# Second norm's tiles of two sequences turned by 32x32 blocks through DRAM, and two early norms moved

## The chip, the cores and the metric

One core of one Trainium2 chip runs the whole program in one launch. The metric is device time in microseconds (us). The engines named are TensorE (PE; its weight loads are shown apart as PEld), VectorE (DVE), ScalarE (ACT), GpSimd (POOL), and SyncE (SP), which here does nothing but issue transfers.

## The reference

Four sequences of 512 tokens with 512 features, float32. A sequence mixing block is followed by an MLP block, each behind a layer norm and with a residual:

```
x = x + attention(layernorm(x))
x = x + mlp(layernorm(x))

attention, 4 heads of 128, chunks of 128 tokens:
  q, k, v = projections of x; k normalised per head
  alpha = sigmoid(...), beta = softplus(...)
  cla = cumsum(log(alpha)) in the chunk
  attn = (q k^T) * beta * exp(cla - cla^T), lower triangle
  y = attn v + (q state) * exp(cla)
  state = state * exp(cla_end) + v^T (k * beta * exp(cla_end - cla))

mlp:  Wg, Wu, Wd dequantised from 4-bit codes and scales, 4096 hidden
  out = (gelu(x Wg^T) * (x Wu^T)) Wd^T
```

## The kernel before, in words

There are B = 4 sequences with NCH = 4 tiles of 128 tokens each, 16 tiles in all. A matrix product needs its features on the partitions, so every normalised tile of 128 tokens by 512 features has to be turned. For the MLP a float32 activation is also split into three parts (hi, lo, mi) that multiply separately.

**Steps.** The attention runs as a counted list of steps p, 12 for each sequence: four of `product_v`, four of `product_q`, four of `product_k`. After the projection of a step, `behind(p)` (L775) emits the chunk work that is due. Chunk (b, n), the n-th of sequence b, gets the three steps from 9 + 3(4b + n) on, so it runs beside the projections of a later sequence. Among those three, p % 3 = 0 prepares the decay, which needs a broadcast load of cumulated gate sums (`load_sums`, L579) and gives the mask `dm`; p % 3 = 1 turns what is waiting (`turn("f")`, `turn("a")`), makes `chunk_scores` and multiplies them with `dm` (L674), and issues loads; p % 3 = 2 makes the chunk's output `yp` (`chunk_sums`, L717 and L719), adds it to the residual tile and stores the sum (`accd`, L727), and in `rest()` starts the next chunk's values and calls `second_norm`. Then come the early `first_norm` calls that the table `early` (L739 to L743) holds for this p, and `settle()`. Each engine works through its instructions in the order in which they are emitted.

**The norms.** `norm` (L330) takes statistics on DVE (L334, L338, L340), an inverse root on POOL (L341), and leaves the rest to `settle()` (L343). There are two ways to turn:

- *On PE.* DVE scales the tile in one operation (L359), and `turn` later transposes four 128x128 blocks into a PSUM bank `tp` (L380), and hands it to `use`.
- *By blocks.* DVE scales it in two halves into an order of 32-column pieces (L349). `cross` (L307) writes the tile (256 KB) to DRAM from SP (L310). One step later SP reads it back in four pieces of 64 KB (L315), so that each 32x32 block lands where it belongs but for its own transposition; three steps after that, at the end of the step, DVE transposes within the blocks (`turn_blocks`, L320, L326). The dictionaries `first_of` and `last_of` hold what is due at the start and at the end of a step.

`first_norm` (attention input, key "a") goes by blocks for all sequences but the first and on PE for that. Some keys of sequences 0 to 2 go by blocks also (way_k). `second_norm` (MLP input, key "f", L402) goes on PE for all 16 tiles. Its `use` takes hi with ACT (L406), lo and mi with DVE (L407, L408), and stores the three from SP to DRAM (`h<-g`, L410); the MLP loads them from there (`x<-h`).

**SP** issues nearly all transfers, in the emitted order. An instruction of SP that waits holds everything behind it.

**The MLP** runs in rounds over slices of 128 hidden columns, and overlaps the end of the attention from about 180 us on.

Of the kernel before, what the change touches and what calls it, by code (L numbers as in the profile page):

```python
# [35 lines left out]
def f32(t):  # L36
    return t.bitcast(F32)
# [3 lines left out]
def tile_gated_linear_attention__then__nvfp4_geglu(  # L41
# [22 lines left out]
    NCH = T // P  # L64
# [56 lines left out]
    one_k = Homes("b", 42, [P, T], two_k)  # L121
# [4 lines left out]
    def heads(t):  # L126
        return t.rearrange("p (h d) -> p h d", d=P)
# [176 lines left out]
    def crossed(t):  # L304
        return t.rearrange("p (w k i) -> p k w i", w=KC, i=32)

    def cross(src, key, use, landing, turning):  # L307

        way = dram.tile([KC, P, P], F32, tag=f"way_{key}", name=f"way_{key}")
        nc.sync.dma_start(way.rearrange("w p m -> p w m"), f32(src).rearrange("p (w m) -> p w m", m=P))  # L310

        def land():
            t = one_k.get(f"way_{key}")
            for a in range(KC):
                nc.sync.dma_start(f32(t)[:, a * P : (a + 1) * P], way[:, a * 32 : (a + 1) * 32, :])  # L315
            last_of.setdefault(turning, []).append(lambda: use(t))

        first_of.setdefault(landing, []).append(land)

    def turn_blocks(t, *to):  # L320

        new = f32(t).rearrange("p (a k i) -> p k a i", a=KC, i=32)
        done = 0
        for part in to:
            n = part.shape[1]
            nc.vector.transpose(part.rearrange("p k (a j) -> p k a j", j=32), new[:, done : done + n])  # L326
            done += n
        one_k.put(t)

    def norm(src, key, use, parts=1, within=None, way=None):  # L330


        st = small.tile([P, 6], F32, tag="st", name=f"st_{key}")
        nc.vector.bn_stats(st, f32(src))  # L334
        if within:
            within()
        mv = small.tile([P, 2], F32, tag="mv", name=f"mv_{key}")
        nc.vector.bn_aggr(mv, st)  # L338
        rs = small.tile([P, 1], F32, tag="rs", name=f"rs_{key}")
        nc.vector.tensor_scalar(rs, mv[:, 1:2], 1e-5, None, ALU.add)  # L340
        nc.gpsimd.tensor_tensor(rs, rs, minus_half[:, :1], ALU.pow)  # L341

        def settle():  # L343

            hn = one_k.get(f"hn_{key}")
            w = D // parts
            if way:
                for c in range(2):
                    nc.vector.tensor_scalar(  # L349
                        crossed(f32(hn)).rearrange("p (c two) w i -> p c two w i", c=2)[:, c],  # L350
                        f32(src).rearrange("p (c w i two) -> p c two w i", c=2, w=KC, two=2)[:, c],
                        mv[:, 0:1], rs, ALU.subtract, ALU.mult,
                    )
                one_k.put(src)
                cross(hn, key, way, place[0] + 1, place[0] + 4)
                one_k.put(hn)
                return
            for cols in (slice(i * w, (i + 1) * w) for i in range(parts)):
                nc.vector.tensor_scalar(  # L359
                    f32(hn)[:, cols].rearrange("p (c two j) -> p c two j", two=2, j=P),  # L360
                    f32(src)[:, cols].rearrange("p (c j two) -> p c two j", two=2, j=P),
                    mv[:, 0:1], rs, ALU.subtract, ALU.mult,
                )
            one_k.put(src)
            turned.append((hn, key, use))

        settled.append(settle)
# [34 lines left out]
    def second_norm(b, n, src):  # L402
        def use(tp):
            g = [one_k.get(f"g{j}_{b}_{n}") for j in range(3)]
            hi, lo, mi = g
            nc.scalar.activation(hi, tp, AF.Copy, scale=HI)  # L406
            nc.vector.tensor_tensor(lo, tp, f32(hi), ALU.subtract)  # L407
            nc.vector.scalar_tensor_tensor(mi, f32(hi), ONE_E, tp, ALU.mult, ALU.subtract)  # L408
            for j in range(3):
                nc.sync.dma_start(  # L410
                    h2d[b][j][:, :, n * P : (n + 1) * P].rearrange("k p t -> p k t"), heads(f32(g[j]))
                )
            one_k.put(*g)

        norm(src, f"f{b}_{n}", use)


    zs, ss = {}, {}
# [289 lines left out]
    def chunk_sums(b, n):  # L708
        add = state_sums(b, n) if b < B - 1 else None
        old = ch.pop("old")  # L710
        one_k.put(v_sb.pop((b, n)))
        dm, vb = ch.pop("dm"), ch.pop("vb")
        qc = ch.pop("qc", None)
        yp = psum(f"yp_{b}_{n}")
        for h in range(H):
            hs = slice(h * P, (h + 1) * P)
            nc.tensor.matmul(yp[:, hs], f32(dm)[:, hs], f32(vb)[:, hs], start=True, stop=(n == 0))  # L717
            if n > 0:
                nc.tensor.matmul(yp[:, hs], f32(qc)[:, hs], f32(old)[:, hs], start=False, stop=True)  # L719
        one_k.put(dm, vb)  # L720
        if n > 0:
            one_k.put(qc, old)
        a = acc.pop((b, n))

        def sums():
            nc.vector.tensor_tensor(f32(a), f32(a), yp, ALU.add)  # L726
            nc.sync.dma_start(accd[b * NCH + n], f32(a))  # L727

        def rest():
            if n + 1 < NCH:  # L730
                chunk_values(b, n + 1)
            second_norm(b, n, a)
            if add:
                add()

        return sums, rest
# [2 lines left out]
    early = {}  # L739
    for b in range(1, B):  # L740
        for n in range(NCH):
            p = 3 * NCH * (b - 1) + 3 * n - 1 if b > 1 else 2 + 3 * min(n, 2)
            early.setdefault(p, []).append((b, n))  # L743
    xs = {}

# [253 lines left out]
    with tc.manual_schedule():  # L999
# [45 lines left out]
        p = 0  # L1045
# [95 lines left out]
```

## Time and profile before

| | us |
|---|---|
| median of 3 runs | 1303.85 (1300.8 to 1305.99) |
| the profiled execution's own time | 1303.89 |
| its span | 1302.2 |

Busy time of each engine over the span:

| engine | us | what is in it |
|---|---|---|
| PE | 1289.4 | 1139 are the MLP's products (L853, L897) |
| DVE | 968.9 | MLP sums and the unpacking of its weights |
| ACT | 452.0 | |
| POOL | 113.6 | nearly all in the first 270 us |

A row of the groups reads: line, engine, operation, output<-inputs, shapes, count | busy us, mean ns of one | idle time of the engine just ahead of it and what ended it. Some rows that bear on the turning:

| row | count | mean ns |
|---|---|---|
| L359 DVE, tile scaled in one (tiles of "f") | 16 | about 546 |
| L349 DVE, half of a tile scaled | 16 in 57 to 175 us | 501 (406 where nothing is beside it) |
| L326 DVE, block transposes of 128x256 | 24 | 404 |
| L326 DVE, of 128x512 | 6 | 701 |
| L310 SP, issue of a write | 18 | 380 |
| L315 SP, issue of a read | 72 | 522 |
| L410 SP, issue of a store of h | 48 | 418 |

In the chain of waits each piece is start, length, and what it was; "SPq" is the time that SP spent on issuing.

### The profile page before, as it was taken

How to read it: one execution, taken by the hardware profiler on the slowest of the kernel's cores; microseconds unless marked ns; L12 is line 12 of the kernel's file. 1: busy time of each engine (PE TensorE's matmuls, PEld its weight loads, DVE VectorE, ACT ScalarE, POOL GpSimd, SP SyncE). 2: the span in 40 equal slices, each digit the busy share in tenths (PEclk: the TensorE clock that was granted, in tenths of full speed). 3: DMA queues.
4: the chain of work that ended last, by engine and by line, in shares of the span. 5: the costliest groups of instructions: out<-in, count | busy, mean ns of one | idle time of the engine just before them, and what ended most of it. 6: DMA issues, size and time to landing. Idle time of an engine off the chain costs nothing.

```text
span 1302.2 us, 17046 instructions
## 1 busy us (share of the span) xinstructions
PE 1289.4 (99%) x5736; PEld 1032.0 (79%) x5736; DVE 968.9 (74%) x1581; ACT 452.0 (35%) x878; POOL 113.6 (9%) x179
## 2 busy tenths in 40 slices
PE   9999999999999999999999999999999999999998
PEld 6567676778888888888888888888888888887886
DVE  3577865888777777777777777777777777777566
ACT  2333335743333333333333333333333333332332
POOL 1536362400000000000000000000000000000000
PEclk9999999999999999999999999999999999999999
DMA  5457677987565656555656565555555555555473
GB/s 195 147 178 195 191 197 214 301 268 235 178 194 178 194 178 194 178 194 179 194 179 193 179 193 179 192 180 192 180 191 181 189 183 189 183 178 198 167 252 127
DMA packets 195383, 250.24 MB, mean 192 GB/s; under 512 B 16672, under 2 KB 93792, under 8 KB 195296
## 3 DMA queue, kind: packets, MB, share of 16 engines
q1 hardware_dynamic: 195296, 249.16, 59.2%
q8 instruction: 45, 0.74, 0.2%
q14 instruction: 42, 0.34, 0.1%
HBM read 191.91 MB, written 57.18 MB: 191 GB/s over the span
## 4 chain that ended last, share of the span: by engine, by line
PE 93%; DMA 3%; DVE 2%; SPq 1%; ACT 1%; issue 0%; POOL 0%; DVEq 0%; ACTq 0%; POOLq 0%
PE pa L853 35%; PE p_d L897 26%; PE pb L853 18%; PE pq L450 4%; PE pk L474 2%; PE pva L425 2%; PE pvb L432 2%; PE yp L717 1%; PE sp L663 1%; PE yp L719 1%; DMA x<-in_x 1%; PE dp L688 1%; DMA pk_d<-in_down_p 1%; PE tp_f L380 0%; DMA x<-h 0%
## 5 line engine op out<-in xcount | busy, mean ns | idle before, releaser
L853 PE MATMUL pa<-x,wgu 128*128 128x512 f32 x2048 | 507.2, 390 | 0.0
L853 PEld LDWEIGHTS pa<-x,wgu 128*128 128x128 f32 x2048 | 384.1, 188 | 79.0
L897 PE MATMUL p_d<-wd,i 128*128 128x512 f32 x1542 | 357.2, 389 | 2.3 <-DVE xr L726 0.6
L897 PEld LDWEIGHTS p_d<-wd,i 128*128 128x128 f32 x1542 | 288.3, 188 | 65.6 <-DVE i L877 2.1
L853 PE MATMUL pb<-x,wgu 128*128 128x512 f32 x1024 | 274.7, 390 | 1.8 <-DMA x<-h 1.8
L858 ACT ACTIVATE t<-pb 128x512 f32<-128x512 f32 x256 | 151.3, 591 | 358.0 <-PE pb L853 353.4
L859 DVE TENSOR_TENSOR t<-pa,t 128x512 f32<-128x512 f32 x256 | 176.6, 690 | 81.2 <-ACT t L858 75.9
L853 PEld LDWEIGHTS pb<-x,wgu 128*128 128x128 f32 x1024 | 192.4, 188 | 42.4 <-DMA x<-h 2.5
L905 DVE SCALAR_TENSOR_TENSOR acc<-p_d,acc 128x512 f32<-128x512 f32 (+1 forms) x137 | 93.4, 682 | 124.8 <-PE p_d L897 123.7
L873 ACT ACTIVATE i<-t 128x512 fp32r<-128x512 f32 x128 | 81.0, 633 | 194.2 <-DVE t L870 189.7
L865 ACT ACTIVATE t<-t 128x512 f32<-128x512 f32 x128 | 81.2, 634 | 136.6 <-DVE t L859 136.5
L877 DVE TENSOR_TENSOR i<-t,i 128x512 fp32r<-128x512 f32 x128 | 88.4, 691 | 25.9 <-ACT i L873 24.1
L909 DVE TENSOR_TENSOR acc<-acc,p_d 128x512 f32<-128x512 f32 x135 | 93.0, 689 | 14.8 <-PE pb L853 0.5
L870 DVE SCALAR_TENSOR_TENSOR t<-t,t 128x512 f32<-128x512 f32 x128 | 88.6, 692 | 4.3
L928 POOL TENSOR_TENSOR acc<-acc,last 128x512 f32<-128x512 f32 x1 | 1.3, 1295 | 1015.0 <-ACT last L927 1015.0
L878 DVE SCALAR_TENSOR_TENSOR i<-i,t 128x512 fp32r<-128x512 f32 x128 | 89.0, 695 | 0.0
L450 PE MATMUL pq<-hT,wq 128*128 128x512 f32 x128 | 57.6, 595 | 0.0
L474 PE MATMUL pk<-wk,hT 128*128 128x512 f32 x128 | 57.4, 593 | 0.0
L450 PEld LDWEIGHTS pq<-hT,wq 128*128 128x128 f32 x128 | 23.6, 191 | 24.1 <-issue 23.9
L474 PEld LDWEIGHTS pk<-wk,hT 128*128 128x128 f32 x128 | 23.3, 191 | 23.9 <-issue 23.9
L183 DVE TENSOR_TENSOR wgu<-wgu,wgu 128x1024 fp32r<-128x1024 f32 x32 | 38.9, 1216 | 0.0
L180 DVE SCALAR_TENSOR_TENSOR wgu<-wgu,w_gu 128x1024 fp32r<-128x1024 f32 x32 | 38.9, 1215 | 0.0
(120 smaller groups left out, 906.0 us busy)
## 6 DMA issues: line engine op xcount, KB each, us to landing
x<-h SPq DMA_DIRECT2D x420, 256.0 KB
acc<-acc SPq DMA_DIRECT2D x256, 256.0 KB
h<-g SPq DMA_DIRECT2D x48, 256.0 KB
x<-in_x SPq DMA_DIRECT2D x16, 256.0 KB
pk_gu<-in_gate_p SPq DMA_DIRECT2D x32, 128.0 KB
sc_gu<-in_gate_s SPq DMA_DIRECT2D x64, 64.0 KB
pk_gu<-in_up_p SPq DMA_DIRECT2D x32, 128.0 KB
sc_gu<-in_up_s SPq DMA_DIRECT2D x64, 64.0 KB
```

What stands on the lines that cost most here:

```text
L450: nc.tensor.matmul(pq, f32(wq[k // 2])[:, k % 2, h * P : (h + 1) * P], f32(hT[b][k // 2])[:, k % 2, :], start=(k == 0), stop=(k == KC - 1),)
L474: nc.tensor.matmul(pk, f32(hT[b][k // 2])[:, k % 2, n * P : (n + 1) * P], f32(wk[k // 2])[:, k % 2, :], start=(k == 0), stop=(k == KC - 1),)
L853: nc.tensor.matmul(o, w3[j][:, k % 2, c * P : (c + 1) * P], x[j * KC + k], start=(j == js[0] and k == 0), stop=(j == js[-1] and k == KC - 1),)
L858: nc.scalar.activation(f32(t), pb, AF.Copy, scale=-1.0 / ONE_E)
L859: nc.vector.tensor_tensor(f32(t), pa, f32(t), ALU.add)
L865: nc.scalar.activation(f32(g), f32(g), AF.Gelu_apprx_tanh, scale=ONE_E)
L870: nc.vector.scalar_tensor_tensor(f32(u), f32(g), ONE_E, f32(u), ALU.mult, ALU.mult)
L877: nc.vector.tensor_tensor(il, f32(u), f32(ih), ALU.subtract)
L878: nc.vector.scalar_tensor_tensor(im, f32(ih), ONE_E, f32(u), ALU.mult, ALU.subtract)
L897: nc.tensor.matmul(banks[key_][:, part], inter[i][j][:, n * P : (n + 1) * P], wd[ms[i] // 2][j][:, ms[i] % 2, part], start=(i == 0 and j i ...
L905: nc.vector.scalar_tensor_tensor(a, banks[n, False, part.start][:, part], ONE_E, a, ALU.mult, ALU.add)
L909: nc.vector.tensor_tensor(a, a, banks[n, True, 0], ALU.subtract)
```

## The change

`second_norm` of sequences 0 and 1 (8 of its 16 tiles) goes by blocks instead of on PE. For it, `norm` gets a `way`: once the tile is back from DRAM, one block transpose on DVE (128x512) writes a tile `h2T` in SBUF, from which `use` takes hi, lo and mi; before, it took them from the PSUM bank. The write is issued in the step in which the norm is settled, the reads in the next, and the transpose, the split and the stores of h come three steps later than before (step p + 5 for a norm at step p, where it was p + 2).

The table `early` moves the first norms of sequence 1: its tiles 0, 1, 2, 3 are normalised at steps 2, 2, 5, 8; before, at 2, 5, 8, 8.

```diff
@@ second_norm
             one_k.put(*g)
 
-        norm(src, f"f{b}_{n}", use)
+        def way(t):
+            whole = one_k.get(f"h2T_{b}_{n}")
+            turn_blocks(t, heads(f32(whole)))
+            use(f32(whole))
+            one_k.put(whole)
+
+        norm(src, f"f{b}_{n}", use, way=way if b < 2 else None)
 
@@ early
-            p = 3 * NCH * (b - 1) + 3 * n - 1 if b > 1 else 2 + 3 * min(n, 2)
+            p = 3 * NCH * (b - 1) + 3 * n - 1 if b > 1 else 2 + 3 * max(n - 1, 0)
```

Lines after L415 of the kernel before stand six lines further down in the changed one.

## The prediction

> **What bounds the kernel now.** I read the page first, then each engine's busy time by stage.
>
> ```profile
> PE 1289.4 (99%) x5736; PEld 1032.0 (79%) x5736; DVE 968.9 (74%) x1581; ACT 452.0 (35%) x878; POOL 113.6 (9%) x179
> ...
> PE 93%; DMA 3%; DVE 2%; SPq 1%; ACT 1%; issue 0%; POOL 0%; DVEq 0%; ACTq 0%; POOLq 0%
> ```
>
> ```profile
> 65.70:180.00 114.30, 113.70 (x526) 77.79 (x527) 85.93 (x205) 44.24 (x142) 54.80 (x82) 1.00 0.68 194
> ...
> 290.00:1302.00 1012.00, 1007.34 (x4440) 832.50 (x4438) 769.37 (x1127) 329.70 (x532) 1.29 (x1) 1.00 0.57 188
> ```
>
> Columns of the second fence: stretch, length, busy PE, PEld, DVE, ACT, POOL, granted clock, DMA share, GB/s. TensorE sets the end: whatever it executes less, or waits less, comes off the time, and whatever it waits more is added. From 290 us on it is busy 1007.34 of 1012 us; the change touches nothing there, so only a shift is carried through. The changed tiles lie between 57 and 175 us, where PE has 0.6 us of idle time, DVE 28.4, ACT 70, POOL 59.5. So engines other than PE have room. SP, which issues the transfers, is not in these columns; the chain of waits shows it:
>
> ```profile
> 48.41 5.49 DMA way_a<-hn_a
> 53.92 0.54 SPq L315
> ...
> 57.40 0.70 SPq L315
> 58.15 0.76 SPq L315
> 58.95 5.13 DMA x<-in_x
> ...
> 64.65 0.69 DVE dm L674
> 65.34 0.36 DVE hT L326
> 65.75 2.05 PE pva L425 x8
> ```
>
> A tile turned "by blocks" is written to DRAM (5.5 us to land), SP waits for that, then issues four reads of 0.52 us each (two tiles, eight reads, here), and a load that stood behind them comes 5.1 us after its issue. PE's products of the next sequence wait for the tile's turn. SP's own waits, 46 to 180 us:
>
> ```profile
> SPq L315 <- DMA way_a<-hn_a: 24.1, 8, 3.9
> ...
> SPq L579 <- DMA rows<-rows: 2.3, 1, 2.3
> ```
>
> I measured the stretches between two way_a writes on SP: 11.9 to 16.6 us long, 12 to 19 issues taking 7 to 12 us; nearly all the rest is the wait for the write (24.1 us). Over 49 to 163 us only some 4 us are idle for other reasons. **SP is full there**; its first real pauses are at 187 to 196 us (2.3 and 6.6 us) and 217 to 226 (7.2 us).
>
> **The change part by part.** The order of instructions built from both kernels shows PE with 32 transposes fewer, DVE with 16 instructions more, POOL as before, SP with 40 DMAs more, eight times one write and four reads.
>
> *Transposes gone.* The eight tiles' share of this row:
>
> ```profile
> L380 PE MATMUL tp_f<-ident,hn_f 128*128 128x128 f32 x32 | 4.8, 273 | 0.0
> L326 DVE STREAM_TRANSPOSE kT<-way_k 128x512 f32<-128x512 f32 x4 | 2.8, 702 | 0.0
> L407 DVE TENSOR_TENSOR g<-tp_f,g 128x512 fp32r<-128x512 f32 x8 | 5.5, 692 | 11.3 <-ACT g L406 11.3
> ```
>
> Busy 4.8 us, but the pipeline overlaps: from the end of the work before to the start of the next, a tile takes 0.43 us (62.12 to 62.56, 78.98 to 79.41). 8 x 0.43 = **3.5 us** off PE; upper end 4.8.
>
> *Third norm of sequence 2 sooner.* Tiles 0 to 3 of that sequence are now normalised at steps 2, 2, 5, 8, not 2, 5, 8, 8. The only visible stall this touches is the one at 65.75 (PE waits 2.1 us, weight load 2.3, for hT): the last two tiles no longer arrive together. Gain **2.3 us**, lower end 0 should what follows be as late (dm at 64.65 stands ahead of it on DVE). It also takes the queue of eight reads apart: one write with its reads leaves SP's crowd for an earlier step, relief 0.38 + 4 x 0.57 = 2.7 us there.
>
> *VectorE.* Per tile: two half normalisations of 0.41 less overlap, 0.74, for one of 0.54, plus a transpose of 0.70 (row above): +0.9 us, 7.2 in all against 28.4 idle: hidden. If that cover fails in front of an hT turn, 0.9 per chunk. The subtractions lo and mi (L407, L408) now read two SBUF tensors, not PSUM and SBUF. The row nearest is the MLP's pair at 251 us, beside a POOL multiply of 1.88: 0.89 and 1.22 instead of 0.69 and 0.68. The Trainium skill, "SBUF — State Buffer", in "SBUF: two separate sides", speaks against the change here: a VectorE operation with two SBUF inputs and a GpSimd one that reads SBUF lock each other out for a whole instruction. POOL is busy 48% of the stretch with operations of about 1 us, so the rule makes 16 x 0.48 x 0.5 = 3.8 us (estimate), the row 16 x 0.48 x 0.37 = 2.8. I take the row; both stay inside the idle time. Behind the waiting lo stands the next hT turn, so a late ACT hi (11.3 us of waits over eight tiles already) holds it up; the scores' multiply now stands ahead of it, which is a relief.
>
> *Where to transpose.* "VectorE: DVE Perf Modes", "Rules for kernel authors", says: a 128x128 transpose on TensorE if PSUM is an acceptable destination, and it was. By engine time the row agrees: 0.43 us of PE against 0.9 of DVE and 2.7 of SP. By the rule the change loses whatever cannot be hidden; by the trace it gains 3.5 us because PE is the full engine. All turns on what SP can hide.
>
> *SP and its queue.* Per tile a write at L310 (0.38 + 0.04) and four reads at L315 (4 x 0.57 = 2.3). The write goes out in a pause before reads of another tile: nothing, or 0.42. The reads are 2.3 us per chunk on a full queue. Their bytes, 0.5 MB a tile at 512 B a packet: 1024 packets of 29 ns are 1.9 us of all 16 engines, raising the DMA share from 0.68 to about 0.81. All later issues of the queue come later: acc stores, hT reads, x loads, the sums for the decay, kT reads. Most have slack: last read to turn 7 to 11 us for way_a, 11 to 12 for way_k, 10 for the residual. The sums do not:
>
> ```profile
> 161.31 0.54 SPq L579 DMA_DIRECT2D sums<-rows  x1
> ```
>
> ```profile
> 167.19 1.28 ACT L608 ACTIVATE dm<-sums,ncla 128x128 f32<-128x128 f32 x4 [4.08 <-DMA sums<-rows]
> ```
>
> ```profile
> 171.35 0.69 DVE L674 TENSOR_TENSOR dm<-sp,dm 128x512 f32<-128x512 f32 x1
> ...
> 172.09 0.94 PE L717 MATMUL yp<-vb,dm 128*128 128x128 f32 x6 [0.56 <-DVE dm L674]
> ```
>
> Sequence 3's first sums already set dm, and dm already stalls PE: no slack at all. Up to that issue six tiles have had their reads: 6 x 2.3 = 13.8 us more. Against it: 4.0 idle, 2.7 relief by the earlier tile, and 2.7 because the h stores of a tile go three steps later and are behind the sums (a run of three took 2.3 at 172.05). 13.8 - 4.0 - 2.7 - 2.7 = **4.4 us** later, with the write's cost up to 6.9, at the lower end nothing. The store of h itself, three steps later, meets no consumer before the MLP's loads, 80 us on.
>
> *Sum.* This is in absolute time: the gains made until then are spent in waiting for SP, since SP doesn't follow PE but its own queue. So yp at 172.09 goes to 176.5. After it one or two tiles' transposes are still saved, 0.43 x 2 = 0.9. Net +4.4 - 0.9 = **+3.5 us**: 1303.9 + 3.5 = **1307.4**. The sum is against the profiled execution, 1303.89 (span 1302.2), which is the median, 1303.85. From 187 us SP's pauses take up its lag; PE's shift stays, as the MLP has no idle time to make it good.
>
> **Rivals.**
> *SP's slack suffices, the gains are kept.* For it: 24 us of its waits are for writes to land, in which other issues could go, and most consumers have 7 us. Against: the waiting read blocks its queue, and the sums have no slack. Time: 1303.9 - 3.5 - 2.3 = 1298.1; with the 0.7 stall at 172.09 gone and transposes at 4.8, 1296.
>
> *The queue's cost counts in full* (slower): at the turn steps, 76 to 172 us, eight times 2.3 + 0.42 = 21.8, less 4.0 and 2.7, is 15.1 us on PE from the chunk where the lag passes the slack of 7 to 11 us, about the fifth tile; less 5.8 gained: 1313. If the added traffic also lengthens landing by 0.9 us a tile, as a share of 0.81 against 0.68 would (4.5 us times 0.13/0.68), 1320. For it: the wait for the write is the longest wait of SP, and there are now 8 more. Against: SP's later pauses.
>
> *DVE becomes the bound*: 0.9 + 0.35 of port per tile in front of hT and dm; eight tiles 10 us, less gains 5.8: 1308. Against: 28 us idle.
>
> *The early norm doesn't remove the stall*: 2.3 dearer than the forecast, 1309.7, if the x tile isn't there at step 2.
>
> **How the numbers follow.** About 0.5% (6.5 us) is what a measurement of this kernel tells from no change. Forecast (net of gain and SP lag, own range 1301 to 1312): 0.40, of which 0.33 same, 0.07 slower. Gains kept 0.18: 0.07 faster (under 1297.4), 0.11 same. SP in full 0.32: slower. DVE 0.07: 0.03 same, 0.04 slower. Early stall 0.03: 0.01 and 0.02. Together 0.07 faster, 0.48 same, 0.45 slower. The range reaches to the first rival's centre and most of the second's, 1298 to 1318, and leaves out some 0.2.
>
> **What would show it.** Right: PE with no transposes of tp_f before 175 us, no wait at 65.75, SP's waits at L315 for way_f added to those for way_a, SP's way_a writes of the last tiles 4 to 8 us later, the sums of sequence 3 issued at 165 to 168, and PE's wait at yp there grown from 0.7 to some 6 to 9 us. Stages from 290 us on of unchanged length. Wrong: those sums issued before 162 (SP had room: first rival), PE stalls at every chunk from 120 us on (second), or DVE near 100% in a chunk with turns queued behind lo. A gain over 6.5 us would be more than the removed work holds.

## The result

| kernel | median, us | ratio to before | 95% interval |
|---|---|---|---|
| before | 1304.11 | 1 | |
| changed | 1315.69 | 1.0097 | 1.0076 to 1.0118 |

The change makes the kernel slower by 1.0%, some 12 us. The profiled execution of the changed kernel has a span of 1313.6 us, 11.4 more than before. These lines of its page answer to those shown of before (busy time by engine; chain of waits by engine):

```profile
PE 1289.5 (98%) x5704; PEld 1028.6 (78%) x5704; DVE 973.3 (74%) x1597; ACT 452.5 (34%) x878; POOL 110.8 (8%) x179
...
PE 88%; DMA 4%; DVE 3%; SPq 2%; issue 1%; ACT 1%; POOL 0%; DVEq 0%; POOLq 0%; ACTq 0%
```

PE has 32 instructions fewer and is no less busy (1289.5 against 1289.4): for one thing, part of its work ran at a lower clock, as will be seen. Its part of the chain fell from 93% to 88%, and DMA, DVE and SP took most of the difference. The stages tell where (columns as in the prediction):

```profile
54.00:65.70 11.70, 11.70 (x64) 10.33 (x63) 8.92 (x23) 3.15 (x12) 11.16 (x17) 1.00 0.54 161
65.70:180.00 114.30, 101.92 (x434) 66.00 (x433) 80.17 (x195) 37.10 (x107) 43.74 (x64) 0.96 0.61 178
```

The idle time ahead of 65.7 us is gone, as intended. In the stretch up to 180 us, where PE idled 0.6 us before, it idles 12.4, and its granted clock (third column from the end) is 0.96. The DMA share there is lower than before (0.61, it was 0.68): over the stretch as a whole, the transfers are not what is full.

Setting the same products of the two traces side by side gives PE's lead or lag at each place, after minus before. (Sequences and chunks are numbered from 0 here, as in the code; the prediction's sequence 2 at the stall of 65.75 and sequence 3 of the sums are b = 1 and b = 2.)

| product | before at, us | lag, us | what ended the wait |
|---|---|---|---|
| pva of b = 1 | 65.75 | -2.95 | |
| sp | 108.55 | -4.37 | |
| yp | 113.77 | -2.35 | DVE dm |
| pva | 129.63 | +4.25 | DVE hT |
| pvb behind it | 131.42 | +5.81 | half clock |
| yp | 156.62 | +6.69 | DVE dm |
| tpk | 161.84 | +9.12 | DVE k |
| sp | 166.15 | +10.42 | half clock |
| yp of chunk (2, 0) | 172.09 | +11.55 | DVE dm |
| yp | 241.62 | +14.09 | DMA x<-h (of pb, just ahead) |
| pb | 274.39 | +11.43 | |

Up to 108 us the change gains just what was worked out: 2.3 us at the stall and 0.44 us per tile after it. From there to 172 us it loses 15.9. (The 2.7 us that come back at the end are largely before's own: it waited 1.4 us for x<-h at 268.4 and ran at half clock for 3.4 us from 269.3 on, the changed kernel doesn't there.) The waits of PE in the changed kernel from 46 to 200 us (line waited for: us in total, times, longest):

```profile
PE pva L431 <- DVE hT L326: 6.8, 1, 6.8
PE yp L723 <- DVE dm L680: 5.1, 3, 1.9
PE tpk L599 <- DVE k L486: 2.2, 1, 2.2
```

The longest, in the timeline of DVE and of PE (start, length, what, and in brackets the idle time and its releaser):

```profile
130.72 0.71 DVE L326 STREAM_TRANSPOSE h2T<-way_f 128x512 f32<-128x512 f32 x1 [6.84 <-DMA h<-g]
```

```profile
133.88 3.51 PE L431 MATMUL pva<-wva,hT 128*128 128x264 f32 x8 [6.77 <-DVE hT L326]
```

The new transpose waits for a *store* of h: the slot that it writes was read by that store. Behind it on DVE stand the subtractions that make lo and mi, and then the hT that PE needs. This names a suspect, the reuse of slots, that the prediction did not have. SP's timeline names the other:

```profile
165.40 1.08 SPq L310 DMA_DIRECT2D way_f<-hn_f  x1
166.57 1.13 SPq L310 DMA_DIRECT2D way_a<-hn_a  x1
167.79 0.72 SPq L569 DMA_DIRECT2D rows<-rows  x1
170.71 2.25 SPq L315 DMA_DIRECT2D way_f<-way_f  x4
173.05 2.94 SPq L315 DMA_DIRECT2D way_a<-way_a  x4
176.10 0.62 SPq L585 DMA_DIRECT2D sums<-rows  x1
```

SP stands idle for 2.2 us until way_f's write has landed, then issues four reads, then way_a's four, and only then the sums of chunk (2, 0): at 176.10, before at 161.31.

### The profile page after: what moved, and what is told of

Same layout as the page of the kernel before. It is cut to its first block, busy times and chain, and to the rows that moved or that the text cites. A ratio compares the mean times of both kernels' runs of the same rounds, so it can differ in the third digit from the quotient of the medians.

```text
span 1313.6 us, 17064 instructions
## 1 busy us (share of the span) xinstructions
PE 1289.5 (98%) x5704; PEld 1028.6 (78%) x5704; DVE 973.3 (74%) x1597; ACT 452.5 (34%) x878; POOL 110.8 (8%) x179
## 4 chain that ended last, share of the span: by engine, by line
PE 88%; DMA 4%; DVE 3%; SPq 2%; issue 1%; ACT 1%; POOL 0%; DVEq 0%; POOLq 0%; ACTq 0%
PE pa L859 35%; PE p_d L903 25%; PE pb L859 17%; PE pq L456 3%; PE pk L480 2%; PE pva L431 2%; PE pvb L438 1%; SPq L315 1%; DMA x<-h 1%; DMA way_f<-hn_f 1%; PE sp L669 1%; PE yp L723 1%; DMA x<-in_x 0%; DMA sc_gu<-in_up_s 0%; PE dp L694 0%
## 5 line engine op out<-in xcount | busy, mean ns | idle before, releaser
L915 DVE TENSOR_TENSOR acc<-acc,p_d 128x512 f32<-128x512 f32 x135 | 92.8, 688 | 14.1
L431 PE MATMUL pva<-wva,hT 128*128 128x264 f32 x128 | 32.9, 402 | 7.8 <-DVE hT L326 7.5
```

The lines of the kernel that those rows point to most:

```text
L915: nc.vector.tensor_tensor(a, a, banks[n, True, 0], ALU.subtract)
```

## The experiments

Two theories: *the queue* (SP's issues and landing waits in series are too long for a chunk, so all that it issues comes late), and *the slots* (h2T and the parts of h take slots out of which a store is still to go). A third, *the way itself*, is that write, landing, reads and turn don't fit in their steps.

### Each part alone

```diff
 e1: way=way if b < 2 else None         and early: 2 + 3 * min(n, 2)
 e2: norm(src, f"f{b}_{n}", use)        and early: 2 + 3 * max(n - 1, 0)
```

> Only the turning by blocks; the early norms stay where they were. The change cost 11.6 us as a whole. If the loss comes from the turning (queue of SP or reuse of slots), the stall at 65.75 (2.3 us) is there again and the loads of three tiles crowd into the same steps: 1316 to 1321, slower than the changed kernel by 2 to 5 us. Rival, that the moved norms did the harm: at or below 1306.

> Only the norms of sequence 1 moved; all second norms on PE as before. By the prediction's step: the stall at 65.75 goes, 1303.9 - 2.3 = 1301.6, no stall comes in its place, and the rest of the profile is the same but for a shift. Rival, that a tile is not loaded at step 2 or its write crowds SP: 1304 or more.

e1: 1318.12 us, 1.0113 (1.0096 to 1.0130). e2: 1299.55 us, **0.9978 (0.9971 to 0.9985)**. The early norms alone gain 0.22%, 3 us: the stall at 65.75 (PE's lead there is 2.2 us), and the small one at 172.09 as well (lead 3.05). The turning alone loses all of it: the two parts add up within their intervals. So everything below is about the turning; e2 is faster than both kernels of this case.

### The slots

e3 passes over slots of h for some steps, e5 every slot that a store has read (shown is e3's choice of a slot; the lines that note the stores are left out).

```diff
-            tag = self.free.pop(0)
+            ripe = [t for t in self.free if clock[0] - self.stored.get(t, -9) > 6]
+            tag = (ripe or self.free)[0]
+            self.free.remove(tag)
```

> The changed kernel, but a free slot is passed over for 6 steps after a store of h went out of it, as long as there is another. In the changed kernel the transpose h2T at 130.72 and mi at 167.82 waited for a store of h, three steps older, out of the slot they took; PE stood for 6.9 and 2.4 us behind them, and its clock was half for some 3.4 us after each, 1.7 us lost each time. If reuse of slots is the cause: both waits go, 12 us less waiting, of which the sums' lateness gives some back, 1303 to 1308. If the queue of SP by itself is the cause: the reads of way_f and way_a are as late, 1312 to 1316.

> The slot rule again, now for every slot that a store reads: those of h, of the sums (accd) and of both kinds of way. e3 passed over h's slots alone, and its h2T work waited for the accd store instead (11.0 us at once). Here no slot that a store read in the last 4 steps is taken while another is free. Slot theory: no wait of h2T, lo or mi for a store is left, PE's stalls of 6.9 and 2.4 us and the two stretches of half clock go: 1303 to 1308. Queue theory: reads or sums are so late that PE stalls as long elsewhere, 1313 to 1318.

e3: 1320.90 us, 1.0136 (1.0120 to 1.0151). e5: 1319.58 us, 1.0115 (1.0095 to 1.0136). Neither is faster than the change. In e3, DVE waited for the store of a residual tile instead (its L412 is lo):

```profile
DVE g L412 <- DMA acc<-xr: 15.0, 2, 11.0
```

In e5 no wait of DVE for a store is left from 46 to 200 us, and PE waits as long elsewhere (15.2 us in all, 14.1 in the change):

```profile
ACT dm L626 <- DMA sums<-rows: 41.2, 5, 11.3
...
PE yp L735 <- DVE dm L692: 10.6, 3, 4.6
```

ACT waits 41.2 us for the sums (32.2 in the change, 21.3 before). The slot theory falls: the wait for a store was where the lag came to light first, and with it gone the lag comes to light at the next thing that SP brings. The store was late because SP was late: an earlier tile's last part of h was ready at 114.0 us and its three stores were issued from 123.94 on; before, for the stores issued from 114.89 on, at 111.0.

### The order on VectorE

```diff
-            last_of.setdefault(turning, []).append(lambda: use(t))
+            (last_f if key[0] == "f" else last_of).setdefault(turning, []).append(lambda: use(t))
...
         do(last_of, p)
+        do(last_f, p)
```

> The changed kernel, with the turn of way_a (hT, kT) put ahead of the turn of way_f, its split and its stores within a step. PE's stalls of 6.9 (133.9 us) and 0.9 (200.5) came for hT behind a waiting h2T on VectorE. If VectorE's order, with reuse of slots, carries the loss: both go with the half clock after the first, 9 us, 1305 to 1309. If SP's lag carries it: hT's stall goes, but k and dm's sums are still late, and PE meets the lag there: 1311 to 1317.

1316.59 us, 1.0106 (1.0091 to 1.0121), as the change. PE's waits from 46 to 200 us:

```profile
PE sp L669 <- DVE kT L326: 7.2, 2, 4.6
PE yp L723 <- DVE dm L680: 4.6, 2, 3.4
...
PE pva L431 <- DVE hT L326: 0.7, 1, 0.7
```

The 6.8 us for hT are 0.7 now, and kT, which comes by SP too, has 7.2. Where before is at 129.63, PE is still 1.75 us ahead, and the change is 4.25 behind; where before is at 172.09, it is 13.6 behind. Again the same lag, met elsewhere.

### The reads at other places

A tile normalised at step p is read back at step p + 2, not in the step next to its write: `place[0]` is p + 1 by then. e4 issues way_f's reads a step later, at p + 3. e6 has besides the turn three steps later, and e5's slots; e7 is e6 with these reads issued by ACT.

For keys "f" alone, in short form:

```diff
 e4: cross(hn, key, way, place[0] + 2, place[0] + 4)
 e6: cross(hn, key, way, place[0] + 2, place[0] + 7)
 e7: reader = nc.scalar if key[0] == "f" else nc.sync
```

> The changed kernel, but the four reads of way_f are issued one step later, behind the reads of way_a and the sums, and so don't wait for their write in front of these; turned at the same step. Queue theory: sums and way_a go out 2.3 us or more (with the wait of up to 2.9 us) earlier, dm's stalls at 111, 163 and 184 us (2.0, 1.8, 1.9) shrink, 1308 to 1312. Slot theory: h2T and mi still wait for the older store, the stalls at 134 and 171 remain, 1312 to 1316.

> The slots of e5, with way_f read one step later (behind way_a's reads and the sums) and turned three steps later, so that it has all the slack that e4 lacked (there h2T waited 25.3 us for its reads). Slot and slack theory: sums go out some 2.3 us earlier than in e5, no stall at a turn; 1299 to 1304. Queue theory in full: SP still issues 40 transfers more, all later loads are late by these, 1308 to 1314.

> e6, but way_f's reads are issued by ACT, which has 70 us idle in the stretch, not by SP: the same bytes, 2.3 us less of SP's queue per tile. If SP's issuing bounds: 2 to 8 us faster than e6, at best 1296 to 1299 (the gains of 3.5 and 2.3 kept). If the traffic or the length of the way bounds: as e6 within 2. If ACT's own waits for the write or issue time stand in front of dm and hi: slower than e6.

e4: 1326.63 us, 1.0183 (1.0168 to 1.0198). e6: 1328.03 us, 1.0185 (1.0164 to 1.0205). e7: 1330.29 us, 1.0196 (1.0174 to 1.0217). The expectations of e4 and e6 were missed. Of e7's, the one that has ACT's own waits in the way is what the profile shows, but its time can't be told from e6's. e4, waits of DVE and PE:

```profile
DVE h2T L326 <- DMA way_f<-way_f: 22.7, 5, 7.7
...
PE sp L669 <- DVE kT L326: 10.7, 3, 5.7
```

The sums are in time (ACT's wait for them is 16.8), but now the way lacks its slack: h2T waits for its own reads, and kT behind it. In e6 it has the slack; but SP's pauses ahead of way_a's reads are back in full (23.5 us), and ACT waits 41.5 us for the sums. Nor did the issues of the 32 reads get cheaper at these places: 30.0 us in e4 and 27.7 in e6, 18.8 in the change. In e7 SP is rid of the reads, but ACT has a queue also, and an issue that waits holds up what PE needs (la, for the decay):

```profile
ACT L561 <- DMA way_a<-way_a: 15.6, 1, 15.6
...
PE rps L579 <- ACT la L561: 17.3, 2, 12.3
```

So e7 doesn't tell what SP's relief alone would bring.

### One read instead of four

```diff
-            for a in range(KC):
-                nc.sync.dma_start(f32(t)[:, a * P : (a + 1) * P], way[:, a * 32 : (a + 1) * 32, :])
+            nc.sync.dma_start(f32(t).rearrange("p (w m) -> p w m", m=P), way.rearrange("w p m -> p w m"))
```

(for keys "f" alone; the edit is shortened). The blocks of these tiles then don't land where they belong, so this run tells what the issues cost and no more.

> The changed kernel with way_f read back in one transfer instead of four: the same 256 KB in the same pieces of 512 B, but three issues of SP (1.7 us) less per tile; the blocks then don't land where they belong, so second norms of sequences 0 and 1 are permuted wrongly. If SP's issuing is what is short: 8 x 1.7 = 13.7 us of its queue come back, dm's sums and h's stores go out earlier, 1301 to 1308. If the traffic or the landing of the way is what is short: 1313 to 1317, as the change.

1301.50 us, 0.9996 (0.9988 to 1.0003): 1.0% faster than the change, with the same bytes in the same pieces (254.49 MB in both traces, 84032 packets of 512 B). The issues of way_f, e8 and the change (count: min/median/max ns):

```profile
L315 SPq DMA_DIRECT2D way_f<-way_f x8: 359/363/432, 69.0 to 173.6; - x8
```

```profile
L315 SPq DMA_DIRECT2D way_f<-way_f x32: 517/522/2197, 67.9 to 187.1; - x32
```

0.36 us of SP per tile, not 4 x 0.57 = 2.3: 15 us over eight tiles, and 13 to 14 us of time came back. This is the run that settles most of it: the bytes, the wait for the write (SP waits 14.8 us at way_f from 46 to 200 us) and DVE's added work are all there, and most of the loss is gone. Not all of it: e2 less the 3.5 us of transposes would be some 1296 (an estimate), so e8 still gives up about 5 us. And it leaves open whether the time of the three issues counts or that three transfers fewer are outstanding.

### Issues alone

```diff
+            if key[0] == "f" and int(key[1]) < 2:
+                few = lambda i: nc.sync.dma_start(tiny[i * 8 : i * 8 + 8, :], xf[i * 8 : i * 8 + 8, :8])
+                few(0)
+                first_of.setdefault(place[0] + 1, []).append(lambda: [few(i) for i in range(1, 5)])
```

> e2 (early norms, all second norms on PE) with five transfers of 256 bytes that nobody reads added per second norm of sequences 0 and 1, at the places in SP's order where the change has its write and its four reads of way_f: the change's issues without its bytes, its wait for the write, its VectorE work or its later stores. If SP's issues alone bring the loss: most of what lies between e2 and the change comes back, 1307 to 1314. If it takes the traffic, the landing or the later turn: 1299 to 1303.

On the kernel of e2. 1300.15 us, 0.9987 (0.9981 to 0.9994): only some 1.2 us more than e2. The expectation of the queue theory was missed, and SP's waits from 46 to 165 us say why, e2 and then e11:

```profile
SPq L315 <- DMA way_a<-hn_a: 22.5, 7, 3.8
```

```profile
SPq L315 <- DMA way_a<-hn_a: 8.2, 7, 4.0
```

The small transfers have nothing to wait for, so SP issues them *in* the pause before way_a's reads, which shrinks by 14.3 us. They are also shorter, 0.31 us in the median against 0.52, and move next to no bytes: e11 adds 9.9 us of issuing to e2's, the change 25.8 (next table). So e11 shows what a pause takes in; it is not the change's issuing at full size. In the change the pause is not filled, it moves to way_f; SP's waits over the same stretch:

```profile
SPq L315 <- DMA way_f<-hn_f: 11.3, 5, 2.9
SPq L315 <- DMA way_a<-hn_a: 4.2, 1, 4.2
```

SP's time from the way_a write of tile (1, 3) (48.9 us before), over the eight writes that follow, added up from the issues in the traces:

| kernel | us | issues | issuing, us | the rest, us |
|---|---|---|---|---|
| before | 114.2 | 130 | 79.4 | 34.8 |
| e2 | 113.1 | 126 | 77.3 | 35.9 |
| e11 | 114.3 | 162 | 87.2 | 27.1 |
| e8 | 119.3 | 138 | 87.4 | 31.9 |
| change | 133.4 | 159 | 103.1 | 30.4 |

In before and e2, PE goes through these eight chunks in 113 to 114 us. e11 fits by filling pauses; the change adds 23.7 us of issuing and keeps all but 4.4 us of the pauses. e8 is over by 5 to 6 us, about what its time gives up.

### Fewer tiles

```diff
 e10: way=way if b < 1 else None
 e9:  way=way if b == 2 else None
```

> The changed kernel with turning by blocks for sequence 0's four tiles alone (chunks from 48 to 105 us). In the changed kernel PE was 4.4 us ahead of before at 104 us and lost 2.0 at 111, 6.9 and 1.6 at 134. If SP's lag adds up from tile to tile: half of the reads, so less than half of the loss, and time to make it good before the sums at 161: 1300 to 1306. If each tile costs its own share: 1303.9 + 11.6 / 2 less half, about 1308 to 1311.

> The early norms, and turning by blocks for sequence 2's four second norms alone, whose chunks run from 165 to 225 us, where SP has pauses of 2.3, 6.6 and 7.2 us. Four tiles' transposes on PE less, 4 x 0.43 = 1.7. If SP's fullness is what costs: e2's 1299.6 less 1.7, about 1298, at most 2 us given back. If turning by blocks loses anywhere (slots, landing): 1301 to 1306.

e10: 1314.51 us, 1.0087 (1.0070 to 1.0104). e9: 1311.62 us, 1.0067 (1.0055 to 1.0080). Both missed: four tiles in either place lose most of what eight lose. In e10 the lag goes on growing after the last of its reads, from +3.2 (at before's 127.85) to +10.2 (172.09): SP, once late, doesn't catch up. Why the lag grows was not taken apart. Two parts show: half clock for 3.4 us from 130.7 on (1.7 us), and the last turned tile's three stores of h, which, put off, are issued beside the next tile's (1.6 us at 142.78). In e9, PE is 4.4 us ahead at 211 us and 8 behind at 270. The pauses of SP that were to hide its reads were, before, mostly these (170 to 290 us):

```profile
SPq L410 <- ACT g L406: 22.8, 6, 7.2
```

A store of h waiting for hi is no room: it ends when ACT is done, and what is queued behind starts then. In e9 SP has 9.2 us of waits of its own at way_f:

```profile
SPq L315 <- DMA way_f<-hn_f: 9.2, 4, 3.6
```

What share of e9's loss is these waits and what the stores' places was not separated.

## Why the prediction was right and wrong

The range (1298 to 1318) holds the time, but only because it was drawn wide enough to take in most of a rival: the likeliest value, 1307.4, was too low by 8 us. What happened is the second rival, the queue's cost in full (1313 to 1320), to which 0.32 was given; the moved norms' gain is inside it.

- *Transposes gone*: right, 0.44 us per tile in the lead up to 108 us (0.43 forecast).
- *Third norm sooner*: right, 2.3 forecast; 3 in e2, since the stall at 172.09 goes as well. The relief of 2.7 us for SP is there as well: in e1, without it, the sums of chunk (2, 0) go out at 178.87, 2.8 us after those of the change. As forecast, the two don't add up in the time: e1 is slower than the change by some 2.4 us, and their intervals overlap.
- *VectorE*: right that it hides: e8 has all of its work, and PE waits 4.4 us there from 46 to 200 us, 3.2 of them for dm. The 2.8 us for lo and mi were not needed: in the change all sixteen took 0.68 to 0.69 us, as before from PSUM, with little of POOL beside them (POOL's operations are 0.67 us in the mean in that stretch of before, not about 1, so the page's rule makes less than the 3.8 us). In e8 one of the sixteen took 1.54, beside a POOL multiply (vb<-v,brn); the rule of the port that the prediction cites, which would make them longer just there, fits that one.
- *SP and its queue*: **the step that failed**, by size. It put the sums of chunk (2, 0) later by 13.8 - 4.0 - 2.7 - 2.7 = 4.4 us; they were later by 14.8 (161.31 to 176.10), and yp by 11.55.

  SP's time from the way_a write of tile (1, 3) to these sums, added up from the issues in the traces, was 112.4 us before and is 128.6 in the change (it starts 1.4 earlier): issuing +20.8, the rest -4.6. The credits were there: 4.6 us of the rest for 4.0; four reads of way_a fewer, 2.16, for the relief of 2.7; and not three but six stores of h that are no longer ahead of the sums (15, it was 21), 4.45 at before's mean, for 2.7.

  What was too small is the cost. The reads ahead of the sums are those of seven tiles, not six (28 issues, 14.74 us and the gaps between them). Their seven writes, put at nothing or at most 2.5, took 4.03. And one term was put at nothing: the 117 issues that both kernels have in this stretch took **8.62 us** more, way_k's 16 reads 0.94 us each in place of 0.70. (The rows of SP in the table of before are medians; the means are higher.) The same difference is 6.5 to 8.5 us in e1, e3, e5 and e12, which have the four reads too, 4.3 in e8, which issues one, and none in e11 (3.2 less), whose transfers are small. So the longer issues come with transfers that move whole tiles, and there are fewer of them where one read stands for four; what makes them longer is open.
- *Slack of 7 to 11 us* for the other loads and "no consumer" for h's stores: wrong in one point. A store has a consumer, the next user of its slot; that is what met the lag at 133.9. But in e5 taking that wait away gained nothing.
- *"PE stalls at every chunk from 120 us on"* was named as the second rival's mark; from 111 us on nearly every chunk has one (111, 134, 163, 171, 184, 200). The sums "issued at 165 to 168" were at 176, and SP's last two way_a writes were 15.4 and 17.9 us later, not 4 to 8. PE's wait at yp of chunk (2, 0) was 1.7 us, not 6 to 9: it had met the lag at earlier products.
- The half clock, some 3 us of the loss (before loses 1.7 to it at another place), was in no case.

## What to carry to other kernels

A queue that issues in order is full when its issues and its waits add up to the period, and a wait is only room for what may be issued ahead of it: put a new transfer's reads into a pause that is there (before the read that waits), not behind a pause of their own. Count issues of four pieces against one of the same bytes, and don't take their length as fixed: in the change the issues that were there already took longer too. When a stall names a late buffer, ask first why the buffer is late: taking that wait away (e3, e5, e12) only moved the same lag to the next thing that SP delivers. A variant that follows from this, way_f's reads three steps later, ahead of the waiting reads of the next way_a, and turned three steps after that, was not tried.

## What the runs showed of the hardware

PE's granted clock fell to a half around idle times. In the changed kernel (stretch, length, busy of PE, PEld, DVE, ACT, POOL, clock, DMA share, GB/s):

```profile
126.00:134.00 8.00, 1.23 (x11) 1.04 (x10) 2.53 (x5) 1.57 (x2) 0.99 (x1) 0.75 0.82 245
134.00:136.00 2.00, 2.00 (x5) 1.59 (x6) 2.00 (x7) 0.00 (x0) 0.00 (x0) 0.50 0.77 232
...
138.00:140.00 2.00, 2.00 (x9) 1.39 (x8) 1.81 (x6) 1.13 (x4) 1.05 (x2) 1.00 0.26 77
```

The half clock lasted from 130.05 to 136.9 us and again from 171.0 for 3.4 us, during which a step of pva took 0.44 us, not 0.22, and one of pk 0.85, not 0.43: half of the 3.0 us from 133.9 on and half of 3.4, so 1.5 and 1.7 us lost. In the 3.41 us just ahead of each, PE was busy 0.47 and 1.25 us; ahead of before's own half clock at 269.27, 1.64. The Trainium skill ("TensorE: Matmul & The Clock Gate", "Part 1: The HAM clock gate") puts half clock down to an idle window of about 3.4 us. Here it began before PE had idled that long: the first 2.9 us into an idle time of 6.8, the second after idle times of 1.6 and 2.2 us with 5.5 us of products between them, before's own after one of 1.4. How much idle time is enough, no run here shows; after the idle time of 2.1 us at 65.75, before, there was none.

The issue of one read of 256 KB took SP 0.36 us in the median (e8), and of each of four reads of 64 KB 0.52 (the change), so the time does not go by the bytes of the transfer. Nor is it fixed for a form: the 32 reads of 64 KB took 18.8 us in the change and 30.0 in e4, where they are issued elsewhere in the queue. And way_k's 24 reads, which before and the changed kernel both have (first before):

```profile
L315 SPq DMA_DIRECT2D way_k<-way_k x24: 517/552/1641, 60.7 to 186.1; - x24
```

```profile
L315 SPq DMA_DIRECT2D way_k<-way_k x24: 522/739/1767, 57.7 to 208.4; - x24
```

The shortest are alike, the median rose from 0.55 to 0.74 us.
